# Moving a batch's division, a tile's update end and the addition of beta in an attention stage that shares its steps with other work

## The chip, the cores and the metric

The kernel runs as one program on one core of a Trainium2 chip. The time is device microseconds (us) of one execution. A core has a matrix engine (TensorE, PE in the profile), a vector engine (VectorE, DVE), an engine for activation functions (ScalarE, ACT), a general engine (GpSimd, POOL), and a sequencer that issues transfers (SyncE, SP). Each takes its instructions in the order in which they were issued to it. Matrix products land in PSUM, in banks of 512 float32 per partition; the rest lives in SBUF, which has 128 partitions.

## The reference

The input is x, 8 batches of 112 tokens of width 512, and a context of 375 rows of width 512 for each batch. Four residual steps follow each other: a masked cross attention straight on the context, a feed forward with ternary weights and activations quantised to 8 bits, a cross attention with 16 heads of width 32, and a feed forward with integer weights. The change lies in the third:

```python
q = proj(hs, Wq, bq, S); k = proj(at, Wk, bk, T); v = proj(at, Wv, bv, T)
scores = clip(q @ k.T / sqrt(32), -50, 50)          # masked keys get -50
probs = softmax(scores)
ctx = probs @ v
delta = rs * (ctx @ Wo.T + bo)                      # rs = clip(residual_scale, 0, 0.3)
delta = (delta - mean(delta)) / sqrt(var(delta) + eps) * gamma + beta
x = x + delta
```

The last feed forward then normalises x again, token by token.

## The kernel before, in words

The 896 tokens lie in SBUF as 7 tiles of 128 tokens (`xs[0]` to `xs[6]`). The queries are held turned, as `qT`: 128 partitions by 4 chunks by 896 tokens, so that a chunk of 128 rows holds four heads of 32. Batches (112 tokens) and tiles (128 tokens) do not coincide: tile i needs the batches up to i + 1.

The attention stage is two nested loops, L957 and L958: 8 batches b, and in each three chunks c of 125 keys. I write (b, c) for one such step. In the stage's block all five engines run in the order in which the program is written (`manual_schedule` with all engines, L853). Before and after it only PE and SP do; the other engines' order is then set by a planner that works from estimated costs.

A step (b, c) is made of these parts:

- `scores` (L899): 32 PE instructions give the scores of 16 heads for 125 keys and 112 tokens, into four PSUM banks of the pool `ps_s`, which has just four. DVE clips the four banks one after the other into SBUF (L910), ACT takes the exponential in place (L911). The next step's scores need the same four banks, so each bank must have been clipped before.
- `fill(1)` (L211): one unit of the keys' and values' projection of a later batch. It is either a K unit (L194) or a V unit (L203), 8 PE instructions each, in a bank of the pool `ps_mm` (two banks), which ACT moves to SBUF (L197, L205). Batch 4 has no unit at c = 2.
- `sums` (L916) of the step before: 32 PE instructions multiply the exponentials with the values into the bank `num`. With c = 2 another 16 sum the exponentials themselves into the bank `den`: first those that `add(b)` had put together, then those of chunk 2. ACT then copies `den` into `rden` (L937) and `num` into `qT` (L938).
- `add(b)` (L893), at the front of step (b, 2): four POOL additions put the exponentials of chunks 0 and 1 together (on DVE for the last batch).
- `divide(b)` (L941): DVE takes the reciprocal of `rden` (L947) and multiplies `qT` with it (L948), in two pieces that are cut at the border of a tile.
- the update of a tile, in three parts. `project_product(i)` (L800) is 8 PE instructions with Wo. `project_begin(i)` (L806) adds the bias on DVE, takes mean and variance there, has POOL find the scale `f` with three rounds of an inverse square root (`rsqrt_pool`, L99, seven small POOL instructions) and one more multiplication (L815), then has POOL add beta to the tile (L816), while DVE centres and multiplies with gamma (L817). `project_end(i)` (L820) adds the result to the tile on DVE (L822), takes mean and variance of the new tile (L824, L825) and has POOL find its inverse square root, `rstd4`.
- `write4(i)` and `transpose4(i)` (L835, L840): DVE normalises the tile, PE turns it, ACT moves one part (L847); a last subtraction on DVE (L848) is kept in the list `later` and issued in the next batch.
- the integer weights of the last feed forward: SP loads pieces of up to 640 columns into two buffers `raw` (L869); `convert_integers` (L873) has ACT square a piece (L880) and POOL convert it (L882). The table `due` (L861) says at which steps this happens. It is issued at the front of a step, behind `add` and ahead of `scores`, and the next loads follow it. A load needs a buffer that POOL has finished with.

Before the change the placement in a batch is this, in the order of the program:

```
(b,0): convert | scores | fill | later, project_end(b-3) | sums(b-1,2)
(b,1): convert | scores | fill | divide(b-1) | sums(b,0)
(b,2): add(b) | convert | scores | fill | sums(b,1) | write4(b-3) | product(b-2), begin(b-2) | transpose4(b-3)
```

`project_end` and `write4` are there from b = 3, `product` and `begin` from b = 2, `transpose4` for b = 3 to 6. After the loop the last division and `project_end(5)` follow, and `project(6)` does all three parts of the last tile inside the last feed forward.

Of the kernel before, what the change touches and what calls it, by code (L numbers as in the profile page):

```python
# [39 lines left out]
NCK = S2 // CK  # L40
# [30 lines left out]
def two_layers(ctx: ExitStack, tc: tile.TileContext, x, ctxT, ctxN, mask0, mask1, w1, w2, w3,  # L71
               wq, wk, wv, wo, bq, bk, bv, bo, gamma, beta, rscale,
               wg, sg, wu, su, wd, sd, out):
    nc = tc.nc
# [22 lines left out]
    xs = [tokens[:, i, :] for i in range(NT)]  # L97

    def rsqrt_pool(v, y, name):  # L99

        bits = stat.tile([P, 1], I32, name=f"{name}_b")
        nc.vector.tensor_scalar(bits, v.bitcast(I32), 1, None, ALU.logical_shift_right)
        nc.vector.tensor_scalar(y.bitcast(I32), bits, -1.0, RSQRT, ALU.mult, ALU.add)
        h = stat.tile([P, 1], F32, name=f"{name}_h")
        nc.gpsimd.tensor_scalar(h, v, -0.5, 1.0, ALU.mult, ALU.mult)
        t = stat.tile([P, 1], F32, name=f"{name}_t")
        for _ in range(3):
            nc.gpsimd.tensor_scalar(t, y, y, h, ALU.mult, ALU.mult)
            nc.gpsimd.tensor_scalar(y, t, 1.5, y, ALU.add, ALU.mult)
# [26 lines left out]
    def moments(srcs, name):  # L136

        r = srcs[0].shape[0]
        mv = small[-1].tile([P, len(srcs), nc.vector.BN_AGGR_DIM], F32, name=f"{name}_mv",
                             bufs=buffers(name))[:r]  # L140
        for j, src in enumerate(srcs):
            bn = small[-1].tile([P, nc.vector.BN_STATS_DIM], F32, name="bn", bufs=4)[:r]
            nc.vector.bn_stats(bn, src)
            nc.vector.bn_aggr(mv[:, j, :], bn)
        return mv
# [15 lines left out]
    def load(pool, src, shape, name, queue=nc.sync, dtype=F32):  # L161
        t = pool.tile(shape, dtype, name=name)
        queue.dma_start(out=t, in_=src)
        return t
# [46 lines left out]
    def fill(n=1):  # L211
        for _ in range(n):
            next(kv_steps, None)
# [501 lines left out]
    beta_s = load(tailp, beta.to_broadcast([P, D]), [P, D], "beta", nc.gpsimd)  # L715
# [82 lines left out]
    updates = {}  # L798

    def project_product(i):  # L800
        updates[i] = ps = ps_mm.tile([P, D], F32, name="mm")
        for kc in range(KC):
            nc.tensor.matmul(ps, lhsT=qT[:, kc, i * P:(i + 1) * P], rhs=wo_s[:, kc, :],  # L803
                             start=(kc == 0), stop=(kc == KC - 1))

    def project_begin(i):  # L806

        d = tailp.tile([P, D], F32, name="d", bufs=2)
        nc.vector.tensor_add(d, updates[i], bo_s)
        mv = moments([d], "ln3")  # L810
        var = stat.tile([P, 1], F32, name="ln3_var")
        nc.vector.tensor_scalar(var, mv[:, 0, 1:2], rs2, LN_EPS, ALU.mult, ALU.add)
        f = stat.tile([P, 1], F32, name="ln3_f")
        rsqrt_pool(var, f, "ln3")
        nc.gpsimd.tensor_scalar(f, f, rs, 1.0, ALU.mult, ALU.mult)  # L815
        nc.gpsimd.tensor_add(xs[i], xs[i], beta_s)  # L816
        nc.vector.scalar_tensor_tensor(d, d, mv[:, 0, 0:1], gamma_s, ALU.subtract, ALU.mult)  # L817
        updates[i] = d, f

    def project_end(i):  # L820
        d, f = updates.pop(i)
        nc.vector.scalar_tensor_tensor(xs[i], d, f, xs[i], ALU.mult, ALU.add)  # L822
        bn = stat.tile([P, nc.vector.BN_STATS_DIM], F32, name="bn", bufs=4)
        nc.vector.bn_stats(bn, xs[i])  # L824
        nc.vector.bn_aggr(mv4[:, i, :], bn)  # L825
        var = stat.tile([P, 1], F32, name="ln4_var")
        nc.vector.tensor_scalar_add(var, mv4[:, i, 1:2], LN_EPS)
        rsqrt_pool(var, rstd4[:, i:i + 1], "ln4")
# [22 lines left out]
    with tc.tile_pool(name="work2", bufs=1, side="right") as work2, \  # L851
# [21 lines left out]
        def convert_integers():  # L873
            for raw, which, half, c, n in loaded:
                if (which, half) not in halves:
                    halves[which, half] = slab("w", F32R)
                t = halves[which, half][:, c:c + n]

                k = pieces.pop()
                nc.scalar.activation(t, raw, AF.Square, bias=zero_point,  # L880
                                     accum_out=squares[:, k:k + 1])
                nc.gpsimd.tensor_scalar(t, raw, -128.0, 1.0, ALU.add, ALU.mult)  # L882
            loaded.clear()
# [9 lines left out]
        def add(b):  # L893
            add = (nc.gpsimd if b in ADD_POOL else nc.vector).tensor_add
            for r in range(NR):
                e, e1 = (sets[(b + c) % NCK][r][:CK] for c in range(2))
                add(e, e, e1)  # L897
# [18 lines left out]
        def sums(b, c, es):  # L916
            if c == 0:
                sums.num = ps_av.tile([P, KC, T], F32, name="num")
            num = sums.num
            v = kvs_of[b][1]  # L920
            if c == NCK - 1:
                den = ps_av.tile([P, KC, T], F32, name="den")
                added = sets[b % NCK]
                for k, of in enumerate((added, es)):
                    for r in range(NR):
                        nc.tensor.matmul(den[r * HD:(r + 1) * HD], lhsT=ones[:CK, :HD],  # L926
                                         rhs=of[r][:CK], start=(k == 0), stop=(k == 1))
            for dc in range(KC):
                for r in range(NR):
                    head = slice((4 * dc + r) * HD, (4 * dc + r + 1) * HD)  # L930
                    nc.tensor.matmul(num[r * HD:(r + 1) * HD, dc, :], lhsT=v[:, c, head],  # L931
                                     rhs=es[r][:CK, dc, :], start=(c == 0 and dc == 0),
                                     stop=(c == NCK - 1 and dc == KC - 1))
            if c == NCK - 1:

                rden = added[0]
                nc.scalar.copy(rden, den)  # L937
                nc.scalar.copy(qT[:, :, b * T:(b + 1) * T], num)  # L938
                rdens[b] = rden

        def divide(b):  # L941

            n = (b + 1) * T - (b + 1) * T // P * P
            for t0, t1 in ((0, T - n), (T - n, T)):
                rden, of = rdens[b][:, :, t0:t1], qT[:, :, b * T + t0:b * T + t1]
                if t1 > t0:
                    nc.vector.reciprocal(rden, rden)  # L947
                    nc.vector.tensor_mul(of, of, rden)  # L948
# [4 lines left out]
        last, rdens, later = None, {}, []  # L953
# [3 lines left out]
        for b in range(B):  # L957
            for c in range(NCK):  # L958
                if c == 2 and b in ADD_POOL:
                    add(b)  # L960
                if (b, c) in due:
                    convert_integers()
                    if counts:
                        load_integers(counts.pop(0))
                es = scores(b, c)
                if c == 2 and b not in ADD_POOL:
                    add(b)
                if c < STEPS[b]:
                    fill(1)
                if c == NCK - 1:  # L970
                    sums(*last)
                if (b, c) == (B - 1, NCK - 1):
                    over = tailp.tile([P, 29], F32, name="over")
                    nc.gpsimd.tensor_scalar(over, squares, WIDE, 1.0, ALU.is_gt, ALU.mult)
                if b == 0 and c > 0:
                    next(folding)
                if c == 0:
                    while later:
                        later.pop()()
                    if b >= 3:  # L980
                        project_end(b - 3)
                elif c == 1 and b >= 1:
                    divide(b - 1)
                elif c == 2:
                    turned = 3 <= b < 3 + GROUPS[0][1]
                    if turned:
                        write4(b - 3)
                    if b >= 2:
                        project_product(b - 2)
                    if b == B - 1:  # L990

                        hits = ps_s.tile([1, 29], F32, name="s")
                        nc.tensor.matmul(hits, lhsT=ones[:, :1], rhs=over, start=True, stop=True)
                        wide = tailp.tile([1, 1], I32, name="wide")
                        nc.vector.tensor_reduce(wide, hits, AX.X, ALU.max)
                    if b >= 2:
                        project_begin(b - 2)
                    if turned:
                        later.append(transpose4(b - 3, ps_mm, "mm"))
                if last and c < NCK - 1:  # L1000
                    sums(*last)
                last = b, c, es

# [201 lines left out]
```

## Time and profile before

| what | value |
|---|---|
| median of 3 runs | 516.82 us (516.54 to 517.11) |
| the profiled execution, its own time | 516.34 us |
| its span, first to last instruction | 514.2 us |
| mean granted PE clock | 0.997 |
| attention stage, about 234 to 395 us | 161 us |
| busy there: PE, DVE, ACT, POOL | 159.6, 124.7, 98.4, 83.3 us |

The profile comes from one execution. A row of the timeline gives start and duration in us, the engine, the line, the operation, the tiles out<-in, the shape, and how many instructions in a row were merged. A pair of brackets at its end gives idle time of that engine ahead of the row, and the engine and line that ended it. Where rows are merged, a wait between the merged instructions is inside the duration. A float32 product shows as two PE instructions. Scores of four heads run beside each other in the rows of the array, so 32 of them take 1.14 us from the first start to the last end when nothing holds them up.

### The profile page before, as it was taken

What the parts mean: (1) busy time and instruction counts of PE and PEld (TensorE: products, weight loads), DVE (VectorE), ACT (ScalarE), POOL (GpSimd) and SP (SyncE); (2) the same over time, 40 slices, a digit from 0 to 9 for tenths busy, and PEclk for the clock granted to TensorE, in tenths of its full rate; (3) what the DMA queues carried; (4) which work ended last, traced back from release to release, by engine and by line L of the source; (5) the groups of instructions that cost most, each with busy time, mean ns of one, the idle gap of its engine ahead of it and who ended that gap; (6) DMA issues with size and microseconds to landing.
All of it is one profiled execution on the core that took longest, in us unless ns stands there. A gap on an engine that the chain in (4) does not pass through costs nothing.

```text
span 514.2 us, 8868 instructions
## 1 busy us (share of the span) xinstructions
PE 502.5 (98%) x3402; PEld 315.8 (61%) x3402; DVE 337.2 (66%) x815; ACT 252.8 (49%) x438; POOL 134.4 (26%) x221
## 2 busy tenths in 40 slices
PE   9999999999999999999999999999999999999995
PEld 6445554455545455696565565555555788889984
DVE  3552548767798987965676688986897753334432
ACT  0326656857565666236675366465665233103310
POOL 0000121110111064211551475674754430000000
PEclk9999999999999999999999999999999999999998
DMA  8998795200120100122421112012320000010001
GB/s 241 347 407 326 268 324 205 80 18 0 61 82 1 60 2 0 45 101 61 162 68 51 62 52 62 3 53 62 98 69 13 20 1 1 20 42 20 1 20 48
DMA packets 13489, 45.77 MB, mean 89 GB/s; under 512 B 2097, under 2 KB 3392, under 8 KB 12288
## 3 DMA queue, kind: packets, MB, share of 16 engines
q1 hardware_dynamic: 11888, 41.43, 23.5%
q0 software_dynamic: 1248, 3.70, 2.2%
q8 instruction: 29, 0.48, 0.4%
q14 instruction: 20, 0.16, 0.1%
q10 hardware_dynamic: 304, 0.01, 0.0%
HBM read 41.46 MB, written 1.84 MB: 84 GB/s over the span
## 4 chain that ended last, share of the span: by engine, by line
PE 47%; DVE 6%; POOL 2%; ACT 1%; DMA 1%; issue 1%; DVEq 0%; POOLq 0%; ACTq 0%
PE s L1045 14%; PE mm L203 8%; PE down L1067 7%; PE mm L803 3%; PE s L905 3%; PE num L931 2%; PE mm L194 2%; DVE e L910 2%; PE den L926 2%; PE mm L740 1%; PE mm L738 1%; DMA raw<-in_wd_dram 1%; PE s L744 1%; DVE e L947 1%; ACT e L911 1%
## 5 line engine op out<-in xcount | busy, mean ns | idle before, releaser
L203 PE MATMUL mm<-wv,cT 128*125 128x512 f32 x192 | 87.6, 599 | 0.0
L194 PE MATMUL mm<-cT,wk 128*128 128x375 f32 x256 | 87.3, 485 | 0.0
L1045 PE MATMUL s<-h4T,w 128*128 128x512 f32 (+1 forms) x352 | 72.6, 367 | 0.2 <-PE num L931 0.2
L1045 PEld LDWEIGHTS s<-h4T,w 128*128 128x128 f32 x352 | 63.5, 188 | 8.8 <-PE num L931 0.4
L910 DVE TENSOR_SCALAR e<-s,upper 125x448 f32<-125x448 f32 x96 | 59.0, 677 | 14.7 <-PE s L905 13.9
L911 ACT ACTIVATE e<-e 125x448 f32<-125x448 f32 x96 | 51.6, 570 | 27.8 <-DVE e L910 27.3
L194 PEld LDWEIGHTS mm<-cT,wk 128*128 128x128 f32 x256 | 46.8, 190 | 27.6 <-issue 1.0
L203 PEld LDWEIGHTS mm<-wv,cT 128*125 128x125 f32 x192 | 34.5, 187 | 38.0 <-issue 36.4
L897 POOL TENSOR_TENSOR e<-e,e 125x448 f32<-125x448 f32 x28 | 33.1, 1213 | 15.8 <-PE num L931 15.8
L1067 PE MATMUL down<-w,gu 128*128 128x512 f32 (+1 forms) x176 | 37.0, 367 | 0.0
L541 PE MATMUL mm<-w_q,q_qT 128*128 128x512 fp8e4 (+1 forms) x168 | 34.8, 361 | 0.8 <-DVE tokens L583 0.4
L439 POOL DMA_DIRECT2D tokens<-x x14 | 10.7, 768 | 90.3 <-DVE x L433 63.0
L1067 PEld LDWEIGHTS down<-w,gu 128*128 128x128 f32 x176 | 29.8, 188 | 5.7
L880 ACT ACTIVATE w<-raw,zero_point 128x640 fp32r<-128x640 int32 (+2 forms) x29 | 22.6, 781 | 20.4 <-DMA raw<-in_wd_dram 9.2
L1053 ACT CAST gu<-gu 128x512 fp32r<-128x512 f32 (+1 forms) x22 | 12.5, 568 | 39.6 <-DVE gu L1051 39.6
L570 POOL TENSOR_SCALAR q<-gu 128x704 bf16<-128x704 f32 x14 | 10.8, 790 | 79.8 <-ACT gu L567 79.8
L882 POOL TENSOR_SCALAR w<-raw 128x640 fp32r<-128x640 int32 (+2 forms) x29 | 20.7, 724 | 36.0 <-ACT w L880 35.8
L905 PE MATMUL s<-qT,kv 32*125 32x112 f32 x768 | 29.4, 280 | 0.6 <-DVE qT L748 0.3
L1051 DVE SCALAR_TENSOR_TENSOR gu<-s,su,gu 128x512 f32<-128x512 f32 (+1 forms) x22 | 15.1, 684 | 21.8 <-PE s L1045 20.6
L905 PEld LDWEIGHTS s<-qT,kv 32*125 32x125 f32 x768 | 24.5, 183 | 7.1 <-issue 5.8
L541 PEld LDWEIGHTS <-q_qT 128*128 128x128 bf16 x168 | 16.3, 98 | 19.7 <-issue 2.5
L931 PEld LDWEIGHTS num<-e,kv 125*32 125x32 f32 x768 | 18.4, 110 | 13.6 <-issue 7.9
(238 smaller groups left out, 798.6 us busy)
## 6 DMA issues: line engine op xcount, KB each, us to landing
cT<-in_ctxT_dram SPq DMA_DIRECT2D x13, 750.0 KB, 6.1
raw<-in_w_dram SPq DMA_DIRECT2D x6, 1408.0 KB, 20.3
cN<-in_ctxN_dram SPq DMA_DIRECT2D x8, 768.0 KB, 4.5
raw<-in_wg_dram SPq DMA_DIRECT2D x8, 320.0 KB, 3.0
raw<-in_wu_dram SPq DMA_DIRECT2D x8, 320.0 KB, 2.9
raw<-in_wd_dram SPq DMA_DIRECT2D x8, 320.0 KB, 3.1
out_dram<-d SPq DMA_DIRECT2D x6, 256.0 KB, 2.0
wk<-in_wk_dram SPq DMA_DIRECT2D x4, 256.0 KB, 4.9
```

The lines of the kernel that those rows point to most:

```text
L194: nc.tensor.matmul(ps[dc], lhsT=wk_s[:, kc, dc * P:(dc + 1) * P], rhs=cT[:, kc, :], start=(kc == 0), stop=(kc == KC - 1))
L203: nc.tensor.matmul(ps, lhsT=cT[:, kc, c * CK:(c + 1) * CK], rhs=wv_s[:, kc, :], start=(kc == 0), stop=(kc == KC - 1))
L541: nc.tensor.matmul(ps[:, :n], lhsT=qT[:, kc, :], rhs=w[:, kc * H + n0:kc * H + n0 + n], start=(kc == 0), stop=(kc == KC - 1))
L880: nc.scalar.activation(t, raw, AF.Square, bias=zero_point, accum_out=squares[:, k:k + 1])
L882: nc.gpsimd.tensor_scalar(t, raw, -128.0, 1.0, ALU.add, ALU.mult)
L897: add(e, e, e1)
L905: nc.tensor.matmul(ss[r][:, dc, :], lhsT=kT[rows, dc, c * CK:(c + 1) * CK], rhs=qT[rows, dc, b * T:(b + 1) * T], start=True, stop=True)
L910: nc.vector.tensor_scalar(e, ss[r], upper[:, c, b:b + 1], -CLIP, ALU.min, ALU.max)
L911: nc.scalar.activation(e, e, AF.Exp, scale=SC1)
L931: nc.tensor.matmul(num[r * HD:(r + 1) * HD, dc, :], lhsT=v[:, c, head], rhs=es[r][:CK, dc, :], start=(c == 0 and dc == 0), stop=(c == NCK ...
L1045: nc.tensor.matmul(ps[:, :n], lhsT=w[:, c:c + P], rhs=h4T[k][:, kc, :n], start=(kc == 0 and k == 0), stop=(kc == KC - 1 and k == 1))
L1067: nc.tensor.matmul(ps, lhsT=gus[k][:, hc, j * P:(j + 1) * P], rhs=w[:, c + n0:c + n0 + n], start=(hc == 0 and k == 0), stop=(hc == HC - 1 ...
```

## The change

Three things move; no operation is added or taken away.

- `sums(b-1, 2)` was the last part of step (b, 0). It now stands right behind that step's `scores`, ahead of `fill`.
- `divide(b-1)` moves from step (b, 1) to step (b, 0), behind `later`. `project_end(b-3)` moves from step (b, 0) to step (b, 1).
- POOL's addition of beta moves from the end of `project_begin(i)` to the front of `project_product(i)`; POOL thus does it ahead of that tile's inverse square root.

After it a batch reads:

```
(b,0): convert | scores | sums(b-1,2) | fill | later, divide(b-1)
(b,1): convert | scores | fill | project_end(b-3) | sums(b,0)
(b,2): add(b) | convert | scores | fill | sums(b,1) | write4(b-3) | beta(b-2), product(b-2), begin(b-2) | transpose4(b-3)
```

```diff
     def project_product(i):
+
+        nc.gpsimd.tensor_add(xs[i], xs[i], beta_s)
         updates[i] = ps = ps_mm.tile([P, D], F32, name="mm")
...
         nc.gpsimd.tensor_scalar(f, f, rs, 1.0, ALU.mult, ALU.mult)
-        nc.gpsimd.tensor_add(xs[i], xs[i], beta_s)
         nc.vector.scalar_tensor_tensor(d, d, mv[:, 0, 0:1], gamma_s, ALU.subtract, ALU.mult)
...
                 if c == 2 and b not in ADD_POOL:
                     add(b)
+                if c == 0 and last:
+                    sums(*last)
                 if c < STEPS[b]:
                     fill(1)
...
                     while later:
                         later.pop()()
-                    if b >= 3:
-                        project_end(b - 3)
-                elif c == 1 and b >= 1:
-                    divide(b - 1)
+                    if b >= 1:
+                        divide(b - 1)
+                elif c == 1 and b >= 3:
+                    project_end(b - 3)
...
-                if last and c < NCK - 1:
+                if c == 1:
                     sums(*last)
                 last = b, c, es
```

## Prediction

> **What bounds the kernel now.** I read the page's head first, then busy time by stage, then the attention stage engine by engine in order of time, and last who waits for whom on PE.
>
> ```profile
> span 514.2 us, 8868 instructions
> PE 502.5 (98%) x3402; PEld 315.8 (61%) x3402; DVE 337.2 (66%) x815; ACT 252.8 (49%) x438; POOL 134.4 (26%) x221
> 234.00:395.00 161.00, 159.56 (x1912) 90.01 (x1915) 124.66 (x210) 98.42 (x200) 83.29 (x138) 1.00 0.21 65
> ```
>
> PE sets the time, and the change gives it no work less. It can only move PE's stalls. Few of these show as idle time, because a stalled scores row is simply longer. Batch 6, whose three units are K units:
>
> ```profile
> 350.62 1.14 PE L905 MATMUL s<-qT,kv 32*125 32x112 f32 x32
> 351.69 2.80 PE L194 MATMUL mm<-cT,wk 128*128 128x375 f32 x8
> 354.42 1.71 PE L926 MATMUL den<-e,ones 125*32 125x448 f32 x16
> 355.94 0.95 PE L931 MATMUL num<-e,kv 125*32 125x112 f32 x32
> 356.82 1.14 PE L905 MATMUL s<-qT,kv 32*125 32x112 f32 x32
> ...
> 361.52 1.48 PE L905 MATMUL s<-qT,kv 32*125 32x112 f32 x32
> ```
>
> A free scores row takes 1.14; 1.48 is a stall of 0.34. The stage's others: 0.81 at (2,0) (267.05, row of 1.95), 0.66 at (3,2) (300.70, row of 1.80), idle 0.43 and 0.34 before the transposes of batches 3 and 4, 0.12 in batch 6. Together 2.7 us: that is all the change can win in this stage. What held (6,2) stands on DVE:
>
> ```profile
> 353.13 2.46 DVE L910 TENSOR_SCALAR e<-s,upper 125x448 f32<-125x448 f32 x4
> 355.50 0.68 DVE L848 TENSOR_TENSOR h4T<-mm,h4T 128x512 fp32r<-128x512 f32 x1
> 357.07 0.88 DVE L822 SCALAR_TENSOR_TENSOR tokens<-d,ln_f,tokens 128x512 f32<-128x512 f32 x1 [0.88 <-POOL tokens L816]
> ...
> 359.37 2.45 DVE L910 TENSOR_SCALAR e<-s,upper 125x448 f32<-125x448 f32 x4
> 361.74 2.14 DVE L947 RECIPROCAL e<-e 128x320 f32<-128x320 f32 x1
> 363.98 0.81 DVE L948 TENSOR_TENSOR qT<-qT,e 128x320 f32<-128x320 f32 x1
> 364.72 0.94 DVE L947 RECIPROCAL e<-e 128x128 f32<-128x128 f32 x1
> 365.69 0.29 DVE L948 TENSOR_TENSOR qT<-qT,e 128x128 f32<-128x128 f32 x1
> ```
>
> The clips of (6,1) end at 361.82, and the scores of (6,2), which need those banks, end at 363.00: 1.17 later, as at (3,2) (301.33 and 302.50). So the measure of a batch is when DVE has done the clips of (b,1), against when PE comes to (b,2). PE takes 10.9 us from (b,0) to (b,2) with two K units (batches 3 and 6), 11.8 with one of each (batch 4), 12.7 with two V units (2, 5, 7). Two more engines matter, ACT and POOL:
>
> ```profile
> 353.85 2.35 ACT L911 ACTIVATE e<-e 125x448 f32<-125x448 f32 x4 [2.03 <-DVE e L910]
> ```
>
> ```profile
> 361.71 0.27 POOL L109 TENSOR_SCALAR rstd<-ln_t,rstd 128x1 f32<-128x1 f32 x1
> 361.93 1.42 POOL L882 TENSOR_SCALAR w<-raw 128x640 fp32r<-128x640 int32 x2
> 363.32 4.77 POOL L897 TENSOR_TENSOR e<-e,e 125x448 f32<-125x448 f32 x4
> 368.05 1.59 POOL L882 TENSOR_SCALAR w<-raw 128x640 fp32r<-128x640 int32 x2
> ```
>
> **The change part by part.** *DVE in step (b,0).* Between the clips of (b,0) and of (b,1) DVE now waits for POOL (0.88) and runs `project_end` (357.07 to 359.37: 2.3). Instead it will wait for `rden` and divide. Sums moved ahead of `fill` are done on PE about 3.8 after (b,0) starts (1.07, 1.53, 0.9 to 1.2), but ACT copies `den` only behind the four exponentials of (b,0), which end at 356.2 here; the copy takes 0.53, so the division starts some 1.1 after the clips' end without `later`'s subtraction, 0.6 after it. The division is 3.1 of reciprocals in two pieces (2.14 + 0.94; 1.34 + 1.74) plus products of 0.8 to 1.6, where POOL's additions run beside them (192 columns: 0.36 without, 1.14 with). Batch 7, with no addition on POOL, has the whole in 4.0 (381.95 to 385.98), and I take 4.0 to 4.15, since the new place has no addition beside it; the bounds are 3.1 and 4.7 (batch 5). That is 4.7 in place of 3.2: the clips of (b,1) end 1.5 us later, counted from the end of the product that releases the batch's first DVE work.
>
> A rule bears on those products. The Trainium skill, "SBUF — State Buffer", section "Who interferes with whom", has a vector instruction with two inputs in SBUF block fully against a GpSimd instruction that reads SBUF, whichever starts first. By it the division's products gain in the new place, and the gamma and tile instructions that will lie beside the moved additions lose, up to one addition (1.14) each. The rows of 0.36 and 1.14 fit it; with one such block in each of batches 3 and 6 the sum would be 2.3 higher.
>
> *POOL.* `project_end`'s inverse square root now stands ahead of `add(b)`. From the start of `project_end` to `var` are 1.9, from there to `rstd4` 2.9 (298.56 to 301.45); then come 4.6 to 4.8 of additions, then the conversions of (b,2) at 0.73 each. Queued behind: `den` of the batch on PE, which needs the additions, and SP's load for the next batch's first step, which needs a `raw` buffer from that conversion. A load lands after 2.0 to 2.2 (128 KB) or 2.7 (256 KB); ACT converts it ahead of the exponentials of (b+1,0). Beta's 1.29 goes from the end to the front of the chain; it ended DVE's waits of 0.9 to 1.5 in batches 3 to 7, which would be gone anyway since `project_end` is a step later. Taken at nothing: `f` is there some 6 after the product's end, and DVE asks for it in the new place some 13 after it, so POOL may come 5 us late to that chain before DVE waits again.
>
> *Each batch*, with the lateness d against the trace before:
>
> - 1: the division (448 columns, 2.94 and 0.6 to 1.0) starts at 256.6; the clips of (1,1) end at 262.9, the scores of (1,2) at 264.05 for 263.45: +0.6. The division no longer sits ahead of the clips of (1,2), so (2,0)'s stall goes: d = -0.3.
> - 2: V units, clips of (2,1) end at 279.9, PE comes at 280.3. No stall.
> - 3: without `later`, clips of (3,0) end at 294.9, exponentials 295.5, `rden` 296.0, division to 300.15, clips of (3,1) to 302.6, scores of (3,2) end at 303.8 for 302.5: d = 1.3. The wait of 0.43 before the transposes goes, for ACT's copy is now early: 0.85.
> - 4: `project_end(0)` starts at 302.5, `rstd4` is there at 307.3, additions to 312.0 (PE wants them at 312.7: in time), first conversion 312.75, load 314.9, ACT's conversion 315.5. So the exponentials of (4,0), ready to start at 314.65, start at 315.5 and end at 317.5. `rden` 318.05, division to 322.3, clips to 324.75, scores of (4,2) end at 325.9 for 323.65: d = 2.25; less the 0.34 before the transposes, 1.9.
> - 5: batch 4 is short (one unit less). `project_end(1)` starts at 324.7, `rstd4` 329.5, additions to 334.1. PE now wants them right behind the scores of (5,0), at 332.1; before, a V unit (3.6) and a later place covered this. Stall 1.9: d = 3.8. Two V units then hide the division.
> - 6: two K units. Product ends at 354.05, clips 356.9 to 359.4, subtraction 360.0, `rden` 360.5, division to 364.7, clips to 367.15, scores of (6,2) end at 368.3 for 363.0: d = 5.3; the 0.12 goes: 5.2.
> - 7: additions of batch 6 end at 376.6 (wanted 377.2), the first conversion at 377.35, the load at 380.05, ACT's conversion at 380.9 in place of exponentials from 379.05; they end at 382.85. Division to 387.5, clips to 389.95, scores end at 391.1, wanted at 389.95: d = 6.3. Batch 7's own addition is on DVE and in time.
>
> *Behind the stage* nothing: its last division, `project_end(5)` and `project(6)` are as before, the last waits for POOL's `f` and not for beta. The planner's order there may shift: PE is idle 0.21 ahead of that stage, which is all there is to win, and DVE's wait of 2.23 for `f` at the last tile, hidden today, is the most that could come to light. I take nothing.
>
> Sum: gains 0.3 net at batches 1 and 2, 0.43, 0.34, 0.12; losses 1.6, 1.4, 1.9, 1.5, 1.15 against the plan of that batch. Some +6.3. On the profiled execution, 516.34 (514.2 and 2.1 around it), that is 522.6; the median of the runs lies 0.5 above it, so 523.1, called 523.
>
> **The rivals.** A measurement of this kernel can tell about 0.2% (1 us) from no change.
>
> 1. Only DVE's delay counts; POOL's additions and the loads stay covered. For it: the additions of batch 4 would have to end 1.9 earlier, before 332.2, and the load for (4,0) and (7,0) 0.9 and 1.9 earlier. Then the losses are 1.6, 0.7 and 1.6 in batches 3, 4, 6, and the sum is +2.7: 519.5.
> 2. More is late: the slack of `den` in batches 3 and 6 is only 0.6 to 0.7, and POOL's slowest addition (1.56) in place of 1.14 overruns it, 0.5 each; products blocked at 0.5 in batches 3, 4, 6 and 7. +2.5 to +3: 526.
> 3. Faster: the stalls of 2.7 go and no new one comes: 514.1. The place is DVE between the clips of (b,0) and (b,1): if division and the wait for `rden` take under 2.8 there, clips are done before PE comes to (3,2) and (6,2). For it speak the V batches, which have this room; against it the reciprocals alone, 3.1.
> 4. Losses and gains cancel within 1 us. With the +1.6 of batch 3 and of batch 6, only a division near 3.3 would do it.
>
> **How the numbers follow.** Forecast 0.45, rival 1 0.25, rival 2 0.18, rival 3 0.07, rival 4 0.05. Slower 0.88, the same 0.05, faster 0.07. Low end: rival 1 with the division 1 us shorter in batches 3 and 6 (its lower bound), 517.5. High end: rival 2 with 0.5 more, for a division at its upper bound: 526.5. Rivals 3 and 4 (0.12) lie below this, and some of rival 2 (about 0.06) above.
>
> **What would show it.** In the profile after: scores rows of (3,2), (4,2), (6,2) and (7,2) of 2 to 4 us; `den` of batch 4 held, its row or its idle time naming POOL's L897; additions behind `rstd4`; no wait of L822 on POOL; reciprocals ahead of the clips of (b,1); products of 0.2 to 0.6. The prediction is wrong if scores rows at (3,2) and (6,2) stay under 1.5, if `rden` comes before the exponentials of (b,0) have ended, or if POOL does its additions before the inverse square root.

## The result and the profile after

The changed kernel takes 523.54 us (median of 4 runs, 522.51 to 528.75) against 516.68 before: 1.0149 times the time, 95% interval 1.0115 to 1.0182. Run once more beside some of the experiments it took 523.39 against 516.53, ratio 1.0138 (1.0120 to 1.0155). The forecast was 523.0, slower. Lines of the file behind the insertion have moved by one to three: L905 is L906 now, L910 L911, L926 L927, L931 L932, L947 L948, L897 L898.

The head of the page after: the span has grown by 8.2, and what counts as PE's busy time by 7.3, though PE has the same work.

```profile
span 522.4 us, 8844 instructions
PE 509.8 (98%) x3402; PEld 319.6 (61%) x3402; DVE 338.9 (65%) x815; ACT 253.6 (49%) x438; POOL 134.5 (26%) x221
```

PE in batch 6 after, in order of time:

```profile
354.37 1.14 PE L906 MATMUL s<-qT,kv 32*125 32x112 f32 x32
355.44 1.71 PE L927 MATMUL den<-e,ones 125*32 125x448 f32 x16
356.97 0.95 PE L932 MATMUL num<-e,kv 125*32 125x112 f32 x32
357.85 2.79 PE L194 MATMUL mm<-cT,wk 128*128 128x375 f32 x8
360.57 1.14 PE L906 MATMUL s<-qT,kv 32*125 32x112 f32 x32
...
365.43 2.90 PE L906 MATMUL s<-qT,kv 32*125 32x112 f32 x32
```

The sums now lie ahead of the K unit, as the change says, and the scores of (6,2) take 2.90 where a free row takes 1.14 and the row before took 1.48. DVE in the same batch shows why:

```profile
356.88 2.45 DVE L911 TENSOR_SCALAR e<-s,upper 125x448 f32<-125x448 f32 x4
359.25 0.68 DVE L849 TENSOR_TENSOR h4T<-mm,h4T 128x512 fp32r<-128x512 f32 x1
360.39 2.15 DVE L948 RECIPROCAL e<-e 128x320 f32<-128x320 f32 x1 [0.46 <-ACT e L938]
362.65 0.58 DVE L949 TENSOR_TENSOR qT<-qT,e 128x320 f32<-128x320 f32 x1
363.15 0.94 DVE L948 RECIPROCAL e<-e 128x128 f32<-128x128 f32 x1
364.12 0.66 DVE L949 TENSOR_TENSOR qT<-qT,e 128x128 f32<-128x128 f32 x1
364.70 2.45 DVE L911 TENSOR_SCALAR e<-s,upper 125x448 f32<-125x448 f32 x4
```

From the start of the clips of (6,0) to that of the clips of (6,1) DVE takes 7.82, where it took 6.24 before. The reader sees the three parts of it: a short wait for ACT's copy of the denominator, the division of 4.3, and no `project_end`. The clips of (6,1) end at 367.15 and the scores that need the banks at 368.33, 1.18 later as before.

The second forecast place, the sums of batch 4, on PE and on POOL:

```profile
331.45 1.14 PE L906 MATMUL s<-qT,kv 32*125 32x112 f32 x32
332.52 2.77 PE L927 MATMUL den<-e,ones 125*32 125x448 f32 x15
```

```profile
326.57 0.19 POOL L105 TENSOR_SCALAR ln_h<-ln_var 128x1 f32<-128x1 f32 x1 [8.40 <-DVE ln_var L828]
...
329.34 4.59 POOL L898 TENSOR_TENSOR e<-e,e 125x448 f32<-125x448 f32 x4
333.89 1.72 POOL L802 TENSOR_TENSOR tokens<-tokens,beta 128x512 f32<-128x512 f32 x1
```

POOL has waited 8.4 for the update's variance, then found its inverse square root, and only then added. The additions end at 333.93, while PE asked for them from 332.52 on. The sums take 3.85 from their start to the V unit's, 2.41 in a batch that does not wait: 1.44 lost. The third place, ACT at (7,0):

```profile
381.10 0.72 ACT L881 ACTIVATE w<-raw,zero_point 128x512 fp32r<-128x512 int32 x1 [4.45 <-DMA raw<-in_wd_dram]
381.73 0.19 ACT L881 ACTIVATION_READ_ACCUMULATOR w<-raw,zero_point 128x1 f32 x1
381.82 1.96 ACT L912 ACTIVATE e<-e 125x448 f32<-125x448 f32 x4
383.68 0.51 ACT L938 COPY e<-den 128x448 f32<-128x448 f32 x1
```

ACT stands 4.45 for the load. DVE had begun its clips at 379.50, so the exponentials come 1.6 late, and with them the denominator's copy and the division.

What the prediction had no term for is in the granted clock. Stretches of the profile after; the columns are stretch, length, busy time of PE, PEld, DVE, ACT and POOL with their instructions, granted clock, share of the transfer engines, GB/s:

```profile
388.00:390.00 2.00, 1.67 (x37) 1.07 (x27) 2.00 (x5) 1.18 (x3) 0.02 (x1) 1.00 0.63 168
390.00:392.00 2.00, 1.87 (x28) 1.59 (x28) 1.93 (x4) 1.98 (x4) 0.00 (x0) 0.77 0.39 145
392.00:394.00 2.00, 2.00 (x4) 0.86 (x4) 1.90 (x7) 1.86 (x6) 1.10 (x4) 0.50 0.00 0
394.00:396.00 2.00, 2.00 (x6) 0.90 (x5) 2.00 (x4) 1.65 (x3) 1.70 (x4) 0.87 0.00 0
```

Behind the stall at (7,2) the clock is at half for 3.4 us, from 391.10 to 394.51, and the V unit there takes 4.88 in place of 3.70.

Lost time by places, from the starts of PE's rows (what a row's start is later than the free spacing, and what a row is longer):

| place | before | after | after, run again |
|---|---|---|---|
| (1,2) | 0 | 0.47 | 0.47 |
| (2,0) | 0.81 | 0 | 0 |
| (3,2) | 0.66 | 1.91 | 2.51, K unit 1.03 |
| transposes, batch 3 | 0.59 | 0 | 0 |
| (4,2) | 0 | 1.59 | 0.56 |
| transposes, batch 4 | 0.50 | 0.66 | 0.65 |
| sums of batch 4 | 0 | 1.44 | 1.44 |
| (6,2) | 0.34 | 1.93 | 1.87 |
| transposes, batch 6 | 0.28 | 0 | 0 |
| (7,2) | 0 | 2.36, V unit 1.18 | 1.61 |
| sum | 3.2 | 11.5 | 10.1 |
| span | 514.2 | 522.4 | 521.0 |

The sums explain both spans within 0.1: 8.3 of 8.2, 6.9 of 6.8. About 1.8 of the first is the clock (0.6 in the scores row, by comparison with 2.75 in the other run, and 1.18 behind it).

### The profile page after: what moved, and what is told of

Same layout as the page of the kernel before. It is cut to its first block, busy times and chain, and to the rows that moved or that the text cites. A ratio compares the mean times of both kernels' runs of the same rounds, so it can differ in the third digit from the quotient of the medians.

```text
span 522.4 us, 8844 instructions
## 1 busy us (share of the span) xinstructions
PE 509.8 (98%) x3402; PEld 319.6 (61%) x3402; DVE 338.9 (65%) x815; ACT 253.6 (49%) x438; POOL 134.5 (26%) x221
## 4 chain that ended last, share of the span: by engine, by line
PE 45%; DVE 7%; POOL 4%; issue 2%; ACT 2%; DMA 1%; POOLq 0%; DVEq 0%
PE s L1048 14%; PE down L1070 7%; PE mm L203 6%; PE mm L805 3%; PE s L906 3%; PE mm L194 3%; PE num L932 2%; DVE e L948 2%; DVE e L911 2%; POOL e L898 2%; PE den L927 2%; PE mm L740 1%; PE mm L738 1%; PE s L744 1%; ACT e L912 1%
## 5 line engine op out<-in xcount | busy, mean ns | idle before, releaser
L203 PE MATMUL mm<-wv,cT 128*125 128x512 f32 x192 | 88.7, 606 | 0.0
L912 ACT ACTIVATE e<-e 125x448 f32<-125x448 f32 x96 | 53.0, 573 | 29.2 <-DVE e L911 28.3
L911 DVE TENSOR_SCALAR e<-s,upper 125x448 f32<-125x448 f32 x96 | 58.9, 675 | 10.0 <-PE s L906 10.0
L906 PE MATMUL s<-qT,kv 32*125 32x112 f32 x768 | 34.2, 283 | 2.0 <-DVE qT L748 0.3
L906 PEld LDWEIGHTS s<-qT,kv 32*125 32x125 f32 x768 | 27.4, 184 | 13.8 <-issue 5.9
L898 POOL TENSOR_TENSOR e<-e,e 125x448 f32<-125x448 f32 x28 | 32.1, 1173 | 13.2 <-PE num L932 13.2
L948 DVE RECIPROCAL e<-e 128x448 f32<-128x448 f32 (+6 forms) x14 | 24.5, 1749 | 7.5 <-ACT e L938 7.5
```

Of the source, the lines that this page charges most:

```text
L203: nc.tensor.matmul(ps, lhsT=cT[:, kc, c * CK:(c + 1) * CK], rhs=wv_s[:, kc, :], start=(kc == 0), stop=(kc == KC - 1))
L906: nc.tensor.matmul(ss[r][:, dc, :], lhsT=kT[rows, dc, c * CK:(c + 1) * CK], rhs=qT[rows, dc, b * T:(b + 1) * T], start=True, stop=True)
L911: nc.vector.tensor_scalar(e, ss[r], upper[:, c, b:b + 1], -CLIP, ALU.min, ALU.max)
L912: nc.scalar.activation(e, e, AF.Exp, scale=SC1)
```

## The experiments

My theory: DVE's chain between the clips of (b,0) and of (b,1) is longer with the division than with the update's end; that holds up PE at (b,2), and by way of the later update's end it makes POOL's additions and the loads behind them late. Rivals: the sums' new place costs by itself; beta's new place costs; only DVE's chain counts and POOL is covered. The update's end was not moved alone; how much of the loss is its own can be read from the run without reciprocals.

**Beta alone.**

```diff
     def project_product(i):
+        nc.gpsimd.tensor_add(xs[i], xs[i], beta_s)
         updates[i] = ps = ps_mm.tile([P, D], F32, name="mm")
...
         nc.gpsimd.tensor_scalar(f, f, rs, 1.0, ALU.mult, ALU.mult)
-        nc.gpsimd.tensor_add(xs[i], xs[i], beta_s)
```

> The kernel before with beta's addition moved and nothing else. My theory: DVE's wait for POOL ahead of the update's end (0.88 in batches 4 to 7, 1.47 in batch 3) goes, the clips of (b,1) end that much earlier, and the stalls of 0.66 at (3,2) and 0.34 at (6,2) go; the 0.43 and 0.34 ahead of the transposes of batches 3 and 4 become smaller or go. So 1.0 to 1.8 us faster than before, about 515.2. A rival, that POOL's addition is only moved ahead of the same chain and the tile's scale comes as late as the sum did: no change, within 0.4 us.

515.39 against 516.75, ratio 0.9977 (0.9962 to 0.9993): faster, as expected. DVE's wait in batch 3 is 0.23 in place of 1.47, and the clips of (3,1) start at 298.33 for 298.87, in a profile whose stage begins 0.7 later:

```profile
296.15 0.75 DVE L822 SCALAR_TENSOR_TENSOR tokens<-d,ln_f,tokens 128x512 f32<-128x512 f32 x1 [0.23 <-POOL ln_f L816]
...
298.33 2.46 DVE L910 TENSOR_SCALAR e<-s,upper 125x448 f32<-125x448 f32 x4
```

The scores rows of (3,2) and (6,2) are no longer held. The stall ahead of batch 4's transposes has grown, from 0.34 of shown idle time to 0.79, now for DVE's normalisation. So this part of the change is a gain by itself, and the loss lies in the other parts.

**Sums alone.**

```diff
+                if c == 0 and last:
+                    sums(*last)
                 if c < STEPS[b]:
                     fill(1)
...
-                if last and c < NCK - 1:
+                if c == 1:
                     sums(*last)
```

> The kernel before with the sums of (b-1,2) behind the scores of (b,0) and nothing else. My theory: DVE's order is the old one, POOL's additions come before the update's inverse square root as before and end 2 us or more before PE wants them, so the move costs nothing and wins nothing: within 0.6 us of before. A rival, that the earlier place of the sums is what makes them late for the additions: 1.5 us or more slower than before, with the rows of the sums of batch 4 longer than 2 us.

516.41 against 516.75, ratio 0.9994 (0.9986 to 1.0003): no change. The rival that the sums' place costs by itself is out.

**Beta back.** The kernel after, with beta behind the inverse square root again (the first diff, turned round).

> The kernel after with beta's addition back behind the inverse square root. My theory: the update's end asks for the tile some 13 us after the product, so the place of beta is hidden in the new order: the same as after within 0.7 us, 523. A rival, that beta ahead of the chain is a part of the loss since it makes POOL late: 1.3 us or more faster than after.

522.60 against 516.75, ratio 1.0111 (1.0090 to 1.0133). That is 0.8 under the second run of the kernel after, a little more than I had allowed, and the intervals overlap. There is a mechanism for a small cost. In the profile after, the gamma instruction ahead of the clips of (4,0) takes 1.77 in place of 0.74, while POOL adds beta:

```profile
313.18 1.77 DVE L818 SCALAR_TENSOR_TENSOR d<-d,ln_mv,gamma 128x512 f32<-128x512 f32 x1
```

```profile
313.12 1.28 POOL L802 TENSOR_TENSOR tokens<-tokens,beta 128x512 f32<-128x512 f32 x1
```

With beta back the instruction takes 0.74 ahead of the clips of (4,0) and of (7,0). In the second run of the kernel after it takes 0.74 and 1.74 there, and the scores rows behind are as long in both: 1.70 at (4,2), and 2.74 with beta back for 2.75 at (7,2). There the late load holds the same step, so the block costs nothing. The rival that it is a main part (1.3 or more) is not borne out; where the 0.8 comes from stays open.

**The move of division and update's end, with the sums in their old place.**

```diff
-                if c == 0 and last:
-                    sums(*last)
...
                         later.pop()()
-                    if b >= 1:
-                        divide(b - 1)
...
-                if c == 1:
+                if last and c < NCK - 1:
                     sums(*last)
+                if c == 0 and b >= 1:
+                    divide(b - 1)
```

> The kernel after with the sums of (b-1,2) back at the end of step (b,0), and the division behind them. The denominator then comes 2.8 or 3.7 later on PE. My theory: the division starts 0.2 (K unit) to 1.2 (V unit) later than in after, so every batch loses that much more at (b,2), batches 2 and 5 too; the sums of batch 4 no longer wait (1.2 to 1.5 back). In all 0 to 2 us slower than after: 523.5 to 525.5. A rival, that the sums' place is what costs: at least 1.5 faster than after.

528.47 against 516.48, ratio 1.0230 (1.0216 to 1.0243): 5 us slower than after, more than I gave it. All seven batches lose at (b,2), the V batches too (the scores take 2.17 at (5,2) and 1.87 at (7,2), where a free row takes 1.14), and the clock falls twice:

```profile
326.17 3.75 PE L906 MATMUL s<-qT,kv 32*125 32x112 f32 x32 [0.18 <-DVE e L911]
329.85 1.72 PE L932 MATMUL num<-e,kv 125*32 125x112 f32 x32
...
370.37 3.58 PE L906 MATMUL s<-qT,kv 32*125 32x112 f32 x32 [1.33 <-DVE e L911]
373.88 3.73 PE L194 MATMUL mm<-cT,wk 128*128 128x375 f32 x8
```

So this division costs more without the early sums, and the move of division and update's end is the part that costs. What I had not reckoned with, besides the clock, is that the exponentials of (6,0) now end 6.6 behind the start of their scores, for 5.6 in the kernel after. ACT waits there for the load until 362.21, and on DVE the gamma instruction takes 1.73 in place of 0.74, again beside POOL's addition of beta: both hold the same step. That is 1.0 of the 1.9 by which (6,2) loses more than in the kernel after.

**No reciprocals.**

```diff
-                    nc.vector.reciprocal(rden, rden)
                     nc.vector.tensor_mul(of, of, rden)
```

> The kernel after with its reciprocals left out (qT is multiplied with the denominator itself). DVE is 2.9 to 3.1 shorter in each step (b,0), and nothing else differs. My theory: DVE's chain from the product to the clips of (b,1) is the root of all: its loss at (3,2) and (6,2), and by way of the update's end also POOL's additions and the loads come 3 us earlier. So no scores row over 1.5, no late sums, the granted clock at 1.0 through the stage, and 513.5 to 515.5, below the kernel before. A rival, that late sums and loads stand on their own, from POOL's new order: 517 to 519, with the sums of batch 4 still over 2 us.

513.31 against 516.48, ratio 0.9941 (0.9924 to 0.9957). No scores row is held in the whole stage. The granted clock stays at 1.00. One thing of the rival has come true: the row of `den` in batch 4 is still over 2 us, and from its start to the V unit pass 3.26, for 2.41 without a wait:

```profile
327.59 2.19 PE L927 MATMUL den<-e,ones 125*32 125x448 f32 x15
```

So 2.9 to 3.1 on DVE per batch, in this place, are worth 10 us of the whole; the held scores rows and the fall of the clock go with them. The late additions are a consequence only in part. Of the 1.44 lost at the sums of batch 4, 0.85 is left: POOL still does the update's inverse square root first, and its additions end at 328.41, where PE asks from 327.59 on. That part belongs to the new place of the update's end, with the sums asked for a unit earlier, and not to the division. The kernel before was not run without reciprocals; all its stalls in this stage come to 3.2.

**No additions on POOL**, in the kernel after and in the kernel before.

```diff
-                if c == 2 and b in ADD_POOL:
-                    add(b)
```

> The kernel after without POOL's additions of the exponentials (the denominator then lacks the second chunk's). It takes away three effects at once: sums of batch 4 that wait for the additions (1.5), loads that wait for the conversion behind them (1.0 at batch 7), and DVE instructions that stand while an addition runs (1.77 and 1.64 in place of 0.74 at L818, about 1.0 each in batches 4, 5 and 7). My theory: 3.5 to 5 us faster than after, and what is left to the kernel before is DVE's delay, 2 to 3.5. A rival, that all of the loss is DVE's longer chain from the division: no more than 1 us faster than after.

> The kernel before without POOL's additions, as the control of that run. My theory: only the division's products get shorter (1.14 and 1.43 in place of 0.36 and 0.5), so a part of the stalls at (2,0) and ahead of the transposes goes: 0.5 to 1.2 us faster than before. A rival, that additions on POOL cost the same wherever they stand: as much faster as the kernel after without them.

After: 521.25 against 516.53, ratio 1.0088 (1.0069 to 1.0107), only 2.1 under the second run of the kernel after (523.39); I had expected 3.5 to 5. Before: 515.92, ratio 0.9992 (0.9982 to 1.0001), 0.6 faster. What was to go is gone: the sums of batch 4 take 1.71, the scores of (7,2) 1.14. But PE has lost time in a new way:

```profile
300.85 3.37 PE L906 MATMUL s<-qT,kv 32*125 32x112 f32 x32
304.14 3.95 PE L194 MATMUL mm<-cT,wk 128*128 128x375 f32 x8
...
364.74 2.89 PE L906 MATMUL s<-qT,kv 32*125 32x112 f32 x32
367.56 4.48 PE L194 MATMUL mm<-cT,wk 128*128 128x375 f32 x8
```

The K units behind both stalls run at a granted clock of 0.50 for a part of their time: 1.16 and 1.69 more than 2.79, and some 0.5 in the first scores row, 3.3 in all. My reckoning of this run was right for the waits and had left that out. That called for a test of its own.

**Work in place of two stalls**, on top of the last kernel.

```diff
+                if c == 2 and b in (3, 6):
+                    filler = ps_av.tile([P, KC, T], F32, name="den")
+                    for _ in range(2):
+                        nc.tensor.matmul(filler, lhsT=ones, rhs=wo_s[:, 0, :KC * T],
+                                         start=True, stop=True)
                 es = scores(b, c)
```

> The kernel after without POOL's additions (the denominator lacks the second chunk's), and with two products of 128x448 into the idle bank of the denominator put ahead of the scores of (3,2) and (6,2): PE then works through most of the 1.76 that it stood there. The kernel without this filler took 521.25, 2.6 more than its stalls add up to, and its K units behind those two stalls took 3.95 and 4.48 in place of 2.79, at a granted clock of 0.5 for some 3.5 us each. My theory: standing for 1.76 lowers the granted clock, and work in its place keeps it at 1.0, so this takes 2 to 3.3 less than without the filler, 518 to 519, although PE has 3.4 us more to do. A rival, that the low clock comes from something else or costs nothing of its own: within 0.7 of 521.25, or slower.

518.62 against 516.48, ratio 1.0033 (1.0020 to 1.0046): 2.6 faster than without the filler, with 3.4 us more work on PE. The granted clock stays at 1.00 through the stage, and the K unit takes 2.79. The mean clock of the five executions is 0.997 to 0.999, that of the four without the filler 0.991 to 0.995:

```profile
301.20 1.77 PE L967 MATMUL den<-wo,ones 128*128 128x448 f32 x4
302.90 1.34 PE L906 MATMUL s<-qT,kv 32*125 32x112 f32 x32
304.17 2.79 PE L194 MATMUL mm<-cT,wk 128*128 128x375 f32 x8
```

So the two stalls are what lowered the clock here, and the lower clock has a price of its own, where nothing behind it was late anyway. What is left over the kernel before, 2.1 (2.7 against the kernel before without additions), is DVE's chain without POOL's additions and without the clock, near the 2.7 that rival 1 of the prediction had for it.

**Three buffers for the integer weights.**

```diff
-                raw = work2.tile([P, PIECE], I32, name="raw", bufs=2)[:, :n]
+                raw = work2.tile([P, PIECE], I32, name="raw", bufs=3)[:, :n]
```

> The kernel after with three buffers for the integer weights in place of two, so that the load for (4,0) and (7,0) need not wait for POOL's conversion behind the additions. My theory: the exponentials of (7,0) start 1.6 us earlier and the row of (7,2) shrinks by about 1.0; in batch 4 nothing, since there DVE itself is late by as much. So about 1 us faster than after, between 0.5 and 1.5. A rival, that the loads are covered: no change.

522.42 against 523.39 of the kernel after, both against 516.53 of the kernel before; ratios 1.0114 (1.0097 to 1.0131) and 1.0138 (1.0120 to 1.0155). The medians differ by the 1.0 expected, but the intervals overlap, so the gain is not clear of noise. ACT no longer waits for a load at (4,0) or (7,0), and the scores of (7,2) take 2.32 in place of 2.75. That row has lost 0.43 and not 1.0, because there too the gamma instruction stands while POOL adds beta (1.76 in place of 0.74): the block, hidden behind the late load before, is next in line.

**What the experiments point to**: beta moved, and the new order in batches 1 and 2 alone, where no update's end is on DVE.

```diff
+                if c == 0 and last and b < 3:
+                    sums(*last)
...
                     if b >= 3:
                         project_end(b - 3)
-                elif c == 1 and b >= 1:
+                    elif b >= 1:
+                        divide(b - 1)
+                elif c == 1 and b >= 3:
                     divide(b - 1)
...
-                if last and c < NCK - 1:
+                if c == 1 or (c == 0 and b >= 3):
                     sums(*last)
```

> Beta's addition moved, and the new placement of sums and division in batches 1 and 2 alone, where no update's end stands in the way; batches 3 to 7 keep the old placement. My theory: the gains of beta alone, and the net 0.3 of batches 1 and 2 (the stall of 0.81 at (2,0) goes, about 0.5 comes at (1,2)): 1.3 to 2.2 faster than before, about 514.9. A rival, that moving sums ahead of the unit costs by itself wherever it is done: slower than beta alone by 0.3 or more.

515.09 against 516.75, ratio 0.9965 (0.9953 to 0.9978), 0.3 under beta alone: (2,0) is free and (1,2) loses 0.47, as forecast. PE's longest stand was now ahead of batch 4's transposes:

```profile
328.41 0.63 PE L844 MATMUL mm<-ident,d 128*128 128x128 f32 x4 [0.78 <-DVE d L837]
```

**The normalisation of tile 1 ahead of the scores of (4,2)**, on top of it.

```diff
+                if (b, c) == (4, 2):
+                    write4(b - 3)
                 es = scores(b, c)
...
-                    if turned:
+                    if turned and b != 4:
                         write4(b - 3)
```

> The kernel with beta moved and the new placement in batches 1 and 2 alone (515.09), with the normalisation of tile 1 put ahead of the scores of (4,2) on DVE. There PE stood 0.78 ahead of the transposes, waiting for it. My theory: 0.5 to 0.8 faster, 514.4, since the clips of (4,2), now 0.54 later, are asked for some 5 us later. A rival, that the wait moves to the exponentials or to the scores of (5,0): no change.

513.95 against 516.48, ratio 0.9955 (0.9941 to 0.9969). Against the kernel before it is 2.5 faster, and the fastest that gives the whole computation. The wait of 0.78 is gone, and some 0.35 of it has moved to the scores of (5,0), as the rival had it:

```profile
326.92 0.60 PE L844 MATMUL mm<-ident,d 128*128 128x128 f32 x4
327.45 1.49 PE L905 MATMUL s<-qT,kv 32*125 32x112 f32 x32
```

The profile thus shows about 0.4 of the 1.1 between the two medians, which were measured against two medians of the kernel before (516.75 and 516.48); the rest is not explained.

## Why the prediction was right

By its own steps:

- *DVE in step (b,0)*: right, in mechanism and size. It had 1.5 more from one clips row to the next; batch 6 shows 1.58 (7.82 for 6.24). The division, which waits for ACT's copy, was forecast to start 0.6 behind the subtraction, and starts 0.46 behind it.
- *Batches 1 and 2*: right. The scores of (2,0) end 0.34 earlier than before against the stage's start; forecast 0.3.
- *Batch 3*: right, smaller than forecast. The stall at (3,2) grew by 1.25, forecast 1.6; the transposes gave back 0.59, forecast 0.43.
- *Batch 4*: 1.59 at (4,2), forecast 1.4. The transposes gave back nothing: 0.66 for 0.50, where 0.34 was to be won. There the step failed. It had `rstd4` at 329.5, and so the normalisation ready before the product's end. `rstd4` came on time, but the normalisation takes 1.34 in place of 0.54 while POOL adds:

```profile
329.41 1.34 DVE L838 TENSOR_SCALAR d<-tokens,mv,rstd 128x512 f32<-128x512 f32 x1 [0.19 <-POOL rstd L109]
```

- *Batch 5*: the sums lose 1.44, forecast 1.9. Mechanism right: additions behind the inverse square root, asked for a unit earlier.
- *Batch 6*: the stall grew by 1.59, forecast 1.5.
- *Batch 7*: 1.61 and 2.36 in two profiles, forecast 1.15. The term that was mis-sized is the load: it was issued when forecast (377.12 for 377.35), but took 4.0 to land in place of 2.7, so ACT had it at 381.10 and not at 380.05. Some 0.5 of that came back, in ACT's conversion and a division of 3.85. Then PE was 0.5 less late than forecast when it came to (7,2), and so stood longer; and the 2.36 holds 0.6 of the clock.
- *POOL, beta at nothing*: the cover was right for the wait, which is gone, and wrong for DVE. The rule on the shared port, weighed in the prediction with one block in each of batches 3 and 6, did come true there in the first profile: 1.77 for 0.74 at the gamma instruction, with beta and not the exponentials beside it. In the second it did ahead of (7,0) alone. The Trainium skill, "SBUF — State Buffer", section "Who interferes with whom", has the second instruction stand until the first has ended, and 313.18 to 314.95 behind an addition from 313.12 to 314.40 fits that within 0.2. It did not add 2.3 to the time, since the late load held the same exponentials anyway, as the rows with beta back show.
- *What can be won*: the 2.7 counted shown idle time ahead of the transposes. From the starts of PE's rows the three waits there are 0.16 longer each, and the stalls of the stage come to 3.2.
- *Missing*: the clock. It cost about 1.8 in the first profile; in the second it fell at (3,2) instead, and of the 1.6 there 1.03 came back at (4,2), which was waiting for DVE and ACT in any case. Of the eight executions of the kernel after, the two at a mean clock of 0.999 or more had spans of 520.6 and 520.4, which is 6.4 and 6.2 over the span before; the sum without a term for the clock was 6.3. The others had 520.4 to 522.4 at 0.994 to 0.998, and 526.6 at 0.990.

So the sum was right as a sum of stalls, in the same places, with errors of up to 0.6 on either side; that without the clock they cancel to about 0.2 is luck. That most of it goes back to the division's place is shown by the run without reciprocals, with the sums and beta alone as controls; 0.85 at the sums of batch 4 is left without them and goes back to the place of the update's end. Rival 1, at 519.5, would have been near the mark without the additions, as the filled kernel shows.

## What to carry to other kernels

In a stage where every engine runs in a written order, ask for each moved piece which instruction behind it releases PSUM banks, and compare the chain from release to release with PE's own time between the two: 1.5 us more per batch, on an engine that is busy two thirds of the time, was the root of most of the 6 us lost. A piece that is moved takes its followers on other engines along, so list what now stands behind the moved wait on each queue. Where one part of a change gains and another loses, try the parts alone: here beta alone and the new order in two of eight batches, with one more DVE instruction moved, gave 2.5 us less than before instead of 7 more.

## What the runs showed of the hardware that I had not expected

A stall of PE of about two microseconds can halve its granted clock for 3.4 us after. In the six profiles of the changed kernel and its close relatives (both of after, beta back, three buffers, without additions, sums in the old place) I count 17 stalls of 1.5 or more at (b,2), and 9 of them, of 1.6 to 3.9, are followed by a stretch at a granted clock of 0.50; the other 8 are of 1.6 to 2.4. No stall in this stage of the kernels near before, all under 1, was followed by one.

The trace shows more of this. All nine stretches are 3.41 long. Where one profile has two, they begin a whole number of 3.413 apart: at 302.89 and 391.64 with beta back (26 times), at 303.11 and 367.96 without additions (19), at 328.03 and 372.40 with the sums in the old place (13). So in these traces the clock changes only on the beats of a fixed count, and where a stall lies against them matters. The stalls of 1.9 at (3,2) and (6,2) in the profile after are cut by a beat (302.35 and 367.21), and the clock stays. The stall of 1.9 at (6,2) without additions lies between two (364.55 and 367.96), and the clock falls at the second. That is not the whole rule: of two stalls of 1.6 between beats, the clock fell behind (7,2) with beta back and stayed behind (4,2) in the profile after. What decides stays open.

The Trainium skill, "TensorE: Matmul & The Clock Gate", section "Part 1: The HAM clock gate (the "warmup" mystery)", has the clock fall to half after an idle window of about 3.4 us, watched in a window that runs freely. The half, the length and the beats fit what was measured here; the stalls that were enough are mostly shorter than that.

And PE given useless work of 1.77 us in place of two such stalls made the kernel without POOL's additions 2.6 us faster. In the kernel that does them it was not tried.
